# Splitting two more aggregates of a two-layer graph attention kernel a second time, with the residual rows prepared in DRAM

## The chip, the cores and the metric

The kernel runs on one core of a Trainium2 chip. The metric is the device time of one execution in microseconds (us). The profile names the engines PE (TensorE, matmuls; PEld is its weight load), DVE (VectorE), ACT (ScalarE), POOL (GpSimd) and SP (SyncE, here used only to start DMAs). "L661" is line 661 of the kernel before.

## The reference

Two graph attention layers over N = 2708 rows of D = 1024 features, all in float32. Cut to what matters:

```python
# layer 0
h = relu(layernorm(x))
f, g = h @ Wf + bf, h @ Wg + bg
attention = softmax(where(adj > 0, relu(f @ g.T), NEG), axis=1)
x = x + attention @ (h @ W0 + bW)
# layer 1
h1 = relu(layernorm(x))
hw = h1 @ W1
e = leaky_relu(hw @ a1 + (hw @ a2).T, 0.2)
attention = softmax(where(adj > 0, e, NEG), axis=1)
return x + relu(attention @ hw)
```

The kernel multiplies attention by h first (the "aggregate") and by the weight matrix after that (the "projection").

## The kernel before, in words

**Tiling.** The 2708 rows are 20 full tiles of 128 rows, taken as NQ = 10 pairs, or NK = 5 pairs of pairs, and a left-over of two more tiles (MONO with 128 rows, TINY with 20). Destination rows of the attention matrix lie along the free dimension, in NP = 5 panels of 576, 576, 532, 512 and 512 columns (p = 0 to 4).

**Products.** Every large matrix product is a Strassen-Winograd product: seven half-size products M1 to M7, some on operands that are sums of blocks. An operand of one of them that is built from h lies ready in DRAM, and is streamed into SBUF in tiles `hc`; the other, built from the softmax numerators of the panel, is made in SBUF by VectorE. Two functions compute an aggregate:

- `aggregate` computes seven unsplit products with `accumulate` (matmuls at L661). One product is 10 pairs x 4 blocks of 128 features = 40 matmuls of h columns, h being half of the panel's width, and reads five `hc` tiles of 512 KB.
- `aggregate_quartered` splits each of the seven products again, into seven inner products (L1067) of 5 pairs of pairs x 2 blocks = 10 matmuls with h/2 columns. Its operands are the quarter sums of h, which lie in `hs2_d`, and the quarter sums of the attention block, which VectorE makes with `make`. Each partial result is collected from PSUM into a tile `V` and added into `gT` by VectorE. Before the change only layer 1's panels 1 to 4 are computed so.

`quarters_of(p, S)` returns the functions that make the sums of columns (`first`, `fifth`, `second`, `fourth`), and the operands.

**DRAM scratch.** `hg_d` holds the operands of layer 0's aggregates, 4 KB in a row for each partition and load; `hr_d` and `hs2_d` hold those of layer 1 and their quarter sums, in runs of 1 KB for each block. `hs_d` holds transposed rows for the scores, `mk_d` masks, `wt_d` sums of weights, `x1_d` the rows that layer 0 puts out.

**Order.** For each panel of layer 0 the program emits: the projection of h to queries (`project_q`), the scores (`scores`), the aggregate and the projection (`project`). They interleave: the queries of panel p + 1 stand between the scores and the aggregate of panel p. Layer 1 follows: for each panel an aggregate and a projection.

**Side work.** Small pieces of work stand in two lists, `later` and `lazy`, each with an assumed cost. `behind(us)` is called between groups of matmuls: it adds `us` to a credit and takes pieces while credit is left, from `lazy` only where `spare` is set and `later` is empty. A piece's loads (`fetch`) are emitted a few pieces ahead. One such piece is a quarter item (`put_quarters`): it reads 512 KB of `hr_d` into a tile `hq`, makes four sums on VectorE and stores 512 KB to `hs2_d`. `quarters_until(m)` takes pieces until product m's are made.

**Queues and buffers.** `load` starts a DMA on SP's queue in program order; `store` starts one on GpSimd's queue, which a scheduler orders. ScalarE starts no loads of this kind. Tiles of `stream(...)` (`hc`, `hq`, `hl`, `w`, and more) share a ring of `strm` buffers, and a new tile waits for the release of the oldest one. Tiles of `slot(...)` share 54 buffers.

**The residual.** `finish0(p)` loads x's rows of each output tile (`x_res`, two halves, each as four loads of 64 KB) and adds the bias with two accumulating DMAs on GpSimd's queue (256 KB each, L1612). It then adds the projection's result, stores to `x1_d`, and starts layer 1's normalisation of these rows.

Of the kernel before, what the change touches and what calls it, by code (L numbers as in the profile page):

```python
# [57 lines left out]
def kernel(  # L58
# [60 lines left out]
    strm = ctx.enter_context(tc.tile_pool(name="strm", bufs=12))  # L119
# [34 lines left out]
    groups = [[q, q + 1] for q in range(0, NQ, 2)]  # L154
    group_of = {q: (i, j) for i, g in enumerate(groups) for j, q in enumerate(g)}
    assert sorted(group_of) == list(range(NQ))
    hg_d = [dram.tile([P, 7, len(g), W], FP, name=f"hg_d{i}") for i, g in enumerate(groups)]
    NK = NQ // 2
    WH = W // 2
    hr_d = dram.tile([P, 7, 2, 2, NK, WH], FP, name="hr_d")  # L160
    hs2_d = dram.tile([P, 7, 4, NK, WH], FP, name="hs2_d")

    def rows_at(m, q):

        return hr_d[:, m, :, q % 2, q // 2]
# [30 lines left out]
    spare, from_slots = [False], [False]  # L196
# [14 lines left out]
    def behind(us, psum_free=False):  # L211
        credit[0] = min(credit[0] + us, 2 * us)
        while later and credit[0] > 0 and (psum_free or not later[0][3]) and (not later[0][4] or later[0][4]()):
            credit[0] -= one()
        while spare[0] and not later and lazy and credit[0] > 0:
            credit[0] -= one(lazy)
# [107 lines left out]
    def pair_h(q, ha, hb):  # L324
# [3 lines left out]
        if q >= NQ - F // 2:  # L328
            s1, s2, s3, s4 = (slot(f"g{i}")[:, :W] for i in range(4))
            for m, h in ((M1, ha[0]), (M2, hb[0]), (M4, hb[1])):  # L330
                store(rows_at(m, q), as_blocks(h))
            on.tensor_tensor(s1, ha[1], hb[1], OP.add)
            on.tensor_tensor(s2, s1, ha[0], OP.subtract)
            for m, h in ((M5, s1), (M6, s2)):
                store(rows_at(m, q), as_blocks(h))

            def rest():
                on.tensor_tensor(s4, hb[0], s2, OP.subtract)
                on.tensor_tensor(s3, ha[0], ha[1], OP.subtract)
                for m, h in ((M3, s4), (M7, s3)):  # L340
                    store(rows_at(m, q), as_blocks(h))
# [7 lines left out]
        for m, h in ((M1, ha[0]), (M2, hb[0]), (M4, hb[1])):  # L349
            store(rows_at(m, q), as_blocks(h))  # L350
        store(rows_at(slice(M5, M6 + 1), q), as_blocks(g1[:n]))
        store(rows_at(slice(M7, M3 + 1), q), as_blocks(g2[:n]))

    def rows_h(q, ha, hb):

        i, j = group_of[q]
        for m, h in ((M1, ha[0]), (M5, ha[1]), (M2, hb[0]), (M4, hb[1])):
            store(hg_d[i][:, m, j], h)
# [3 lines left out]
    def sums_h():  # L362

        def fetch(q, two):
            i, j = group_of[q]
            for m in (M1, M2):
                two.append(stream("hr", (P, 2, W)))
                load(two[-1], hg_d[i][:, m:m + 2, j])
# [6 lines left out]
        def second(q, two):  # L375
# [3 lines left out]
            i, j = group_of[q]  # L379
            store(hg_d[i][:, M6:M7 + 1, j], two[0])  # L380
            store(hg_d[i][:, M3, j], b0)
            store(hg_d[i][:, M5, j], b1)
# [6 lines left out]
    BY_QUARTERS = (M1, M5, M2, M6, M7, M3, M4)  # L389
    made_quarters = {}  # L390

    def put_quarters(m, k, to=lazy):
# [3 lines left out]
        def fetch():  # L396
# [5 lines left out]
            for h in range(2):  # L402
                nc.gpsimd.dma_start(two[h], hr_d[:, m, h, :, k])

        def go():
# [5 lines left out]
            for h in range(2):  # L411
                store(hs2_d[:, m, 2 * h:2 * h + 2, k], two[h])
            made_quarters[m] = made_quarters.get(m, 0) + 1
        put(1.7, go, fetch, to=to)

    def quarters_until(m):
        while made_quarters.get(m, 0) < NK:
# [466 lines left out]

    def aggregate(l, p, S, sm, then={}, rate=3.0):
# [28 lines left out]
        def left(m, q, d):  # L914
            i, j = group_of[q]
            if (m, i) not in hc:
                hc[m, i] = stream("hc", (P, 4, WH) if l else (P, 2, W))
                load(hc[m, i], hr_d[:, m, :, :, i].rearrange("p h f c -> p (h f) c") if l else hg_d[i][:, m])
            return hc[m, i][:, d // 2 * 2 + j, d % 2 * P:(d % 2 + 1) * P] if l else hc[m, i][:, j, d * P:(d + 1) * P]
# [67 lines left out]
    def quarters_of(p, S):  # L987
# [9 lines left out]
        def operand(m, q):  # L997
            if m in (M5, M4):
# [30 lines left out]
        def second():  # L1029
            for q in range(NQ):  # L1030
                sub(wa_(q)[:, lo], wb_(q)[:, hi], t1(q))
            for q in range(NQ):
                sub(wa_(q)[:, hi], wb_(q)[:, hi], wa_(q)[:, hi])

        def fourth():
            for q in range(NQ):
                sub(t1(q), wb_(q)[:, lo], wa_(q)[:, lo])
        return {"make": make, "right": right, "first": first, "fifth": fifth, "second": second, "fourth": fourth}

    def aggregate_quartered(p, S, sm, of_right, then={}, fine=1.2):  # L1040
# [12 lines left out]
        def product(m, n, ps, start):  # L1053
            quarters_until(m)
# [782 lines left out]
```

## Time and profile before

| | us |
|---|---|
| median of 3 runs | 3091.45 (3090.53 to 3099.64) |
| the profiled execution, its own time | 3099.78 |
| its span, first to last instruction | 3098.0 |
| TensorE busy | 3002.8 |
| VectorE busy | 2070.7 |
| ScalarE, GpSimd busy | 463.2, 506.3 |
| layer 0's aggregates of panels 1, 2, 3 | 148.1, 137.1, 132.0 |
| layer 1's aggregates of panels 2, 3 | 127.4, 125.0 |

The mean granted TensorE clock is 0.989. The core's DMA queues moved 764.7 MB, 247 GB/s over the span. A busy time is the sum over an engine's instructions; a stage's length is read off the timeline, from its first to its last matmul. The profile's DMA share is the mean busy share of the core's 16 DMA engines in a slice of time, and comes out a few per cent above 1 in the fullest slices. A float32 matmul leaves two records in the trace, so counts of matmul records are twice those of the code.

### The profile page before, as it was taken

Reading aid. Unit: us, or ns where it says so; the run is one execution under the profiler, and the core shown is the slowest. Engines: PE = TensorE matmul, PEld = TensorE weight load, DVE = VectorE, ACT = ScalarE, POOL = GpSimd, SP = SyncE. Lnnn points to the kernel's source line nnn. Section 1 sums busy time; section 2 is a strip of 40 time slices with the busy share of each in tenths; the row PEclk is TensorE's granted clock in tenths of the full one; section 3 lists DMA queues with packets and bytes.
Section 4 is the critical chain, followed back from the end, with each engine's and each line's share of the span. In section 5 each row is a group of like instructions: output and inputs, shape, how many; then the busy total and the mean of one; then the engine's idle time right before and its main releaser. Section 6 shows DMA issues by size and latency. Waiting matters only on the chain.

```text
span 3098.0 us, 41680 instructions
## 1 busy us (share of the span) xinstructions
PE 3002.8 (97%) x14630; PEld 2298.1 (74%) x14630; DVE 2070.7 (67%) x4615; ACT 463.2 (15%) x817; POOL 506.3 (16%) x786
## 2 busy tenths in 40 slices
PE   8998999899999999999999999997999999999998
PEld 4576777657877588885888886783777969879694
DVE  5767693776651596716975277766968768887853
ACT  3420020010110101101011001301222121212200
POOL 1421101310011110214101001141202010020202
PEclk9999999999999999999999999998999999999999
DMA  6999967998565796758967577789667868888896
GB/s 225 291 257 254 301 247 253 309 274 229 178 238 153 217 260 223 244 158 241 278 199 255 164 217 234 237 266 350 229 216 249 274 202 296 287 269 294 264 297 246
DMA packets 448577, 764.70 MB, mean 247 GB/s; under 512 B 175776, under 2 KB 262592, under 8 KB 448368
## 3 DMA queue, kind: packets, MB, share of 16 engines
q1 hardware_dynamic: 393008, 598.31, 62.0%
q0 software_dynamic: 55360, 163.73, 16.4%
q8 instruction: 116, 1.90, 0.3%
q14 instruction: 93, 0.76, 0.1%
HBM read 627.95 MB, written 133.91 MB: 246 GB/s over the span
## 4 chain that ended last, share of the span: by engine, by line
PE 71%; DVE 11%; DMA 7%; issue 7%; SPq 2%; POOL 1%; ACT 1%; POOLq 0%; DVEq 0%; ACTq 0%
PE sz L1378 6%; PE gx L661 6%; PE gy L661 6%; PE gz L661 5%; PE gz L1067 5%; PE pz L1267 4%; PE sx L1378 4%; PE sy L1378 4%; PE px L1267 4%; PE py L1267 3%; PE gx L1067 3%; PE gy L1067 3%; PE M_ps L574 3%; PE qz L661 2%; PE qx L661 2%
## 5 line engine op out<-in xcount | busy, mean ns | idle before, releaser
L1378 PE MATMUL sz<-B,As 128*128 128x288 f32 (+2 forms) x1200 | 293.5, 394 | 11.8 <-DVE st L45 8.8
L1378 PEld LDWEIGHTS sz<-B,As 128*128 128x128 f32 x1200 | 227.8, 191 | 61.8 <-DVE st L45 12.7
L1378 PE MATMUL sx<-B,As 128*128 128x288 f32 (+2 forms) x800 | 199.6, 392 | 6.4 <-DMA As<-hs_d 4.4
L1378 PE MATMUL sy<-B,As 128*128 128x288 f32 (+2 forms) x800 | 199.3, 392 | 2.3 <-DMA As<-hs_d 2.3
L661 PE MATMUL gz<-Sa,hc 128*128 128x288 f32 (+2 forms) x800 | 189.2, 397 | 6.3 <-DMA hc<-hg_d 6.3
L661 PEld LDWEIGHTS gz<-Sa,hc 128*128 128x128 f32 x800 | 153.8, 193 | 40.1 <-DMA hc<-hg_d 6.8
L1378 PEld LDWEIGHTS sx<-B,As 128*128 128x128 f32 x800 | 151.3, 190 | 40.1 <-DMA As<-hs_d 3.7
L1378 PEld LDWEIGHTS sy<-B,As 128*128 128x128 f32 x800 | 152.0, 190 | 33.4 <-issue 2.7
L1067 PE MATMUL gz<-quarter,hc 128*128 128x128 f32 (+2 forms) x1344 | 168.8, 279 | 3.8 <-DVE gT L45 3.7
L143 POOL DMA_DIRECT2D out_dram<-x_res x180 | 89.0, 501 | 482.1 <-DVE x_res L45 474.7
L1067 PEld LDWEIGHTS gz<-quarter,hc 128*128 128x128 f32 x1344 | 160.6, 191 | 5.1 <-DVE gT L45 4.6
L1267 PE MATMUL px<-w,gT 128*128 128x512 f32 x320 | 143.9, 602 | 7.5 <-DMA w<-in_L_gnn_W_dram 6.0
L1267 PE MATMUL pz<-w,ps 128*128 128x512 f32 x320 | 142.1, 594 | 0.8 <-DVE pt L45 0.8
L1267 PE MATMUL py<-w,ps 128*128 128x512 f32 x320 | 142.0, 593 | 0.0
L143 POOL DMA_DIRECT2D mk_d<-mask x55 | 35.8, 652 | 534.8 <-DVE mask L45 528.1
L1267 PEld LDWEIGHTS px<-w,gT 128*128 128x128 f32 x320 | 60.9, 193 | 80.9 <-issue 74.7
L1267 PEld LDWEIGHTS pz<-w,ps 128*128 128x128 f32 x320 | 60.2, 190 | 77.1 <-issue 70.7
L1267 PEld LDWEIGHTS py<-w,ps 128*128 128x128 f32 x320 | 60.5, 190 | 75.8 <-issue 73.9
L574 PE MATMUL M_ps<-wgT,wfT 128*128 128x512 f32 x256 | 113.5, 600 | 1.6 <-ACT hsT L45 1.6
L661 PE MATMUL gy<-T,hc 128*128 128x288 f32 (+2 forms) x480 | 111.6, 394 | 0.0
L977 POOL TENSOR_TENSOR gT<-gT,rr 128x2304 f32<-128x2304 f32 (+5 forms) x12 | 44.4, 3700 | 382.4 <-DVE rr L45 179.8
L661 PEld LDWEIGHTS gy<-T,hc 128*128 128x128 f32 x480 | 91.2, 190 | 19.5
(377 smaller groups left out, 5803.6 us busy)
## 6 DMA issues: line engine op xcount, KB each, us to landing
hc<-hg_d SPq DMA_DIRECT2D x175, 512.0 KB
As<-hs_d SPq DMA_DIRECT2D x150, 512.0 KB
hc<-hr_d SPq DMA_DIRECT2D x119, 512.0 KB
hc<-hs_d SPq DMA_DIRECT2D x112, 512.0 KB
w<-wt_d SPq DMA_DIRECT2D x96, 512.0 KB
w<-in_L_gnn_W_dram SPq DMA_DIRECT2D x72, 512.0 KB
md<-md_d SPq DMA_DIRECT2D x56, 512.0 KB
adj_i<-in_adj_dram SPq DMA_DIRECT2D x200, 128.0 KB
```

What stands on the lines that cost most here:

```text
L143: nc.gpsimd.dma_start(a, b)
L574: nc.tensor.matmul(ps, wfT[a][c // NH][:, c % NH, :], wgT[b][c], start=(c == 0), stop=(c == NC - 1))
L661: nc.tensor.matmul(ps[d], left(m, k, d), right(m, k), start=(start and k == 0), stop=(k == K - 1), skip_group_check=True)
L977: nc.gpsimd.tensor_tensor(of(e, s), of(e, s), by(s, k), OP.mult)
L1067: nc.tensor.matmul(ps[:, d], lhs[:, d * P:(d + 1) * P], inner_right(m, n, k), start=(start and k == 0 and d == 0), stop=(k == NK - 1), ski ...
L1267: nc.tensor.matmul(ps, left[i][m][:, k, :], w_[k], start=(start and k == 0), stop=(k == NH - 1), skip_group_check=True)
L1378: nc.tensor.matmul(ps[:n, :h], lefts[q][:, i % 2, c, :n], B[m][c // 2][:, c % 2, :h], start=(start and c == 0), stop=(c == NH - 1), skip_g ...
```

## The change

1. Layer 0's aggregates of panels 2 and 3 go through `aggregate_quartered`. M1 and M5 stay unsplit there, by way of `accumulate`; the other five products are split into seven inner ones. For layer 0, `V` is one tile of the stream ring, whose buffers grow from 4096 to 4608 bytes a partition; the ring has 11 of them for 12.
2. Layer 0's operands are laid out like layer 1's (`hr_d[0]` for `hg_d`, runs of 1 KB), and have quarter sums of their own (`hs2_d[0]`). Their 25 quarter items enter `lazy` after panel 0's aggregate.
3. During layer 0's aggregates the reads of quarter items, layer 1's among them, are started on ScalarE's queue in program order, instead of on GpSimd's.
4. The residual rows are copied from x to `x1_d` in tile order by DMA from DRAM to DRAM (`copy_residual`, 512 KB a tile as 4 x 32 rows), and the bias is added there by an accumulating DMA (`bias_residual`, 512 KB a tile). `finish0` then needs two loads of 256 KB a tile and no accumulation.
5. `behind` takes at most one piece from `lazy` per call.
6. In `quarters_of`, `second` and `fourth` build their sums in place; the operand of M4 lies in another tile, and `fourth` moves from M2 to M6. Each has as many instructions as before.

The core of the diff:

```diff
-    strm = ctx.enter_context(tc.tile_pool(name="strm", bufs=12))
+    strm = ctx.enter_context(tc.tile_pool(name="strm", bufs=11))
...
-    hg_d = [dram.tile([P, 7, len(g), W], FP, name=f"hg_d{i}") for i, g in enumerate(groups)]
-    hr_d = dram.tile([P, 7, 2, 2, NK, WH], FP, name="hr_d")
-    hs2_d = dram.tile([P, 7, 4, NK, WH], FP, name="hs2_d")
...
+    hr_d = [dram.tile([P, 7, 2, 2, NK, WH], FP, name=f"hr{l}_d") for l in range(2)]
+    hs2_d = [dram.tile([P, 7, 4, NK, WH], FP, name=f"hs2{l}_d") for l in range(2)]
+
+    def rows_at(l, m, q):
+
+        return hr_d[l][:, m, :, q % 2, q // 2]
...
         while later and credit[0] > 0 and (psum_free or not later[0][3]) and (not later[0][4] or later[0][4]()):
             credit[0] -= one()
-        while spare[0] and not later and lazy and credit[0] > 0:
+        if spare[0] and not later and lazy and credit[0] > 0:
             credit[0] -= one(lazy)
...
     def rows_h(q, ha, hb):
 
-        i, j = group_of[q]
         for m, h in ((M1, ha[0]), (M5, ha[1]), (M2, hb[0]), (M4, hb[1])):
-            store(hg_d[i][:, m, j], h)
+            store(rows_at(0, m, q), as_blocks(h))
...
-    BY_QUARTERS = (M1, M5, M2, M6, M7, M3, M4)
+    BY_QUARTERS = [(M2, M6, M7, M3, M4), (M1, M5, M2, M6, M7, M3, M4)]
     made_quarters = {}
 
-    def put_quarters(m, k, to=lazy):
+    def put_quarters(l, m, k, to=lazy):
...
             for h in range(2):
-                nc.gpsimd.dma_start(two[h], hr_d[:, m, h, :, k])
+                (tc.keep_in_program_order(nc.scalar.dma_start(two[h], hr_d[l][:, m, h, :, k])) if reads_by_act[0] else
+                 nc.gpsimd.dma_start(two[h], hr_d[l][:, m, h, :, k]))
...
             for h in range(2):
-                store(hs2_d[:, m, 2 * h:2 * h + 2, k], two[h])
-            made_quarters[m] = made_quarters.get(m, 0) + 1
+                store(hs2_d[l][:, m, 2 * h:2 * h + 2, k], two[h])
+            made_quarters[l, m] = made_quarters.get((l, m), 0) + 1
...
         def operand(m, q):
-            if m in (M5, M4):
+            if m == M5:
                 return t1(q)
             s = wa_(q) if m in (M1, M6, M7) else wb_(q)
...
         def second():
             for q in range(NQ):
-                sub(wa_(q)[:, lo], wb_(q)[:, hi], t1(q))
+                sub(wa_(q)[:, hi], wb_(q)[:, hi], wa_(q)[:, hi])
             for q in range(NQ):
-                sub(wa_(q)[:, hi], wb_(q)[:, hi], wa_(q)[:, hi])
+                add(wa_(q)[:, lo], wa_(q)[:, hi], wa_(q)[:, lo])
 
         def fourth():
             for q in range(NQ):
-                sub(t1(q), wb_(q)[:, lo], wa_(q)[:, lo])
-        return {"make": make, "right": right, "first": first, "fifth": fifth, "second": second, "fourth": fourth}
-
-    def aggregate_quartered(p, S, sm, of_right, then={}, fine=1.2):
+                sub(wb_(q)[:, lo], wb_(q)[:, lo], wa_(q)[:, lo])
+        return {"make": make, "right": right, "operand": operand, "first": first, "fifth": fifth, "second": second, "fourth": fourth}
+
+    def aggregate_quartered(l, p, S, sm, of_right, then={}, fine=1.2, rate=3.0):
 
...
-        before_next = {M1: lambda: make(M5), M5: with_second, M2: lambda: (of_right["fourth"](), make(M6)), M6: lambda: make(M7),
+        before_next = {M1: lambda: make(M5), M5: with_second, M2: lambda: make(M6), M6: lambda: (of_right["fourth"](), make(M7)),
                        M7: lambda: make(M3), M3: lambda: make(M4)}
+        def sums_of_columns():
+            of_right["second"]()
+            inverse.append(inverse_sums(p, sm))
+
+        def collected():
+            if l == 0:
+                t = stream("V", (P, NH, HX))
+                return [t[:, 2 * r:2 * r + 2, :h] for r in range(2)]
+            return [v[:, :, :h] for v in in_pairs("V")]
+
+        if l == 0:
+            hc = {}
+
+            def left(m, q, d):
+                if (m, q // 2) not in hc:
+                    hc[m, q // 2] = four_rows(l, m, q // 2)
+                return hc[m, q // 2][:, d // 2 * 2 + q % 2, d % 2 * P:(d % 2 + 1) * P]
+
+            def first_product(d, ps):
+                nc.scalar.copy(quad(0, lo)[:, d], ps)
+                nc.scalar.copy(quad(1, lo)[:, d], ps)
+            exps_until(NQ)
+            of_right["fifth"]()
+            accumulate(left, of_right["operand"], NQ, h, (M1, M5), then,
+                       {M1: first_product, M5: lambda d, ps: add(quad(0, hi)[:, d], ps, quad(0, lo)[:, d])}, "g",
+                       {M5: sums_of_columns}, rate=rate, by_k=True, more={(M5, NQ // 2): with_second})
+
         left_out = None
-        for m in BY_QUARTERS:
-            V = [quad(*direct[m])[:, 2 * r:2 * r + 2] for r in range(2)] if m in direct else [v[:, :, :h] for v in in_pairs("V")]
+        for m in BY_QUARTERS[l]:
+            V = [quad(*direct[m])[:, 2 * r:2 * r + 2] for r in range(2)] if m in direct else collected()
             c11, c12 = (V[0][:, :, b * hb:(b + 1) * hb] for b in range(2))
             c21, c22 = (V[1][:, :, b * hb:(b + 1) * hb] for b in range(2))
             X = bank2("gx")
@@ -1169,9 +1194,7 @@
                 into_place(m, V, 1)
                 scale(m, 1)
             if m == M5:
-                of_right["second"]()
-            if m == M5:
-                inverse.append(inverse_sums(p, sm))
+                sums_of_columns()
...
                 fetch(q + 2)
+            if p and q in (2, 6):
+                (copy_residual if q == 2 else bias_residual)(p)
             sa, sb = slot("Sa"), slot("Sb")
...
+    def tiles_of(p):
+        return list(full(p)) + ([MONO, TINY][p - 1:p] if p in (1, 2) else [])
+
+    def copy_residual(p):
+        for t in tiles_of(p):
+            if t < MONO:
+                r = places[t][0][1]
+                nc.gpsimd.dma_start(x1_d[t].rearrange("(g r) c -> g r c", g=P // B32),
+                                    bass.AP(tensor=x.tensor, offset=x.offset + r * D, ap=[[P * D, P // B32], [D, B32], [1, D]]))
+            else:
+                for ps, r in places[t][:1] if t == TINY else places[t]:
+                    nc.gpsimd.dma_start(x1_d[t][:NY] if t == TINY else x1_d[t][ps],
+                                        x[r:r + ps.stop - ps.start, :])
+
+    def bias_residual(p):
+        for t in tiles_of(p):
+            n = NY if t == TINY else P
+            nc.gpsimd.dma_start(x1_d[t], bass.AP(tensor=bw.tensor, offset=bw.offset, ap=[[0, n], [1, D]]), accum_op=OP.add)
 
     def finish0(p):
...
                 xs[t] = row_halves("x_res", t == MONO)
-                load_rows_of(t, xs[t], x)
                 for e in range(2):
-                    nc.gpsimd.dma_start(xs[t][e], bias_of_W(e * W, P, W), accum_op=OP.add)
+                    load(xs[t][e], x1_d[t][:, e * W:(e + 1) * W])
...
+    SPLIT_EARLY = (2, 3)
...
-            hooks[M1] = lambda: (take_max(0), sums_until(3))
+            hooks[M1] = lambda: (take_max(0), sums_until(3), copy_residual(0))
+            hooks[M5] = lambda: bias_residual(0)
...
-        spare[0], from_slots[0] = p > 0, p == NP - 1
-        G[p] = aggregate(0, p, S, got["sm"], then)
-        spare[0] = False
+        spare[0], from_slots[0], reads_by_act[0] = p > 0, p == NP - 1, True
+        if p in SPLIT_EARLY:
+            G[p] = aggregate_quartered(0, p, S, got["sm"], quarters_of(p, S), then)
+        else:
+            G[p] = aggregate(0, p, S, got["sm"], then)
+        spare[0] = reads_by_act[0] = False
         if p == 0:
             flush()
+            for m in BY_QUARTERS[0]:
+                for k in range(NK):
+                    put_quarters(0, m, k)
             ahead[0] = 2
...
```

## The prediction

> **What bounds the kernel now.** I read the page from the top: busy times first, then the chain that ended last, then the groups of instructions.
>
> ```profile
> PE 3002.8 (97%) x14630; PEld 2298.1 (74%) x14630; DVE 2070.7 (67%) x4615; ACT 463.2 (15%) x817; POOL 506.3 (16%) x786
> ...
> DMA  6999967998565796758967577789667868888896
> ...
> PE 71%; DVE 11%; DMA 7%; issue 7%; SPq 2%; POOL 1%; ACT 1%; POOLq 0%; DVEq 0%; ACTq 0%
> ...
> L661 PE MATMUL gz<-Sa,hc 128*128 128x288 f32 (+2 forms) x800 | 189.2, 397 | 6.3 <-DMA hc<-hg_d 6.3
> ...
> L1067 PE MATMUL gz<-quarter,hc 128*128 128x128 f32 (+2 forms) x1344 | 168.8, 279 | 3.8 <-DVE gT L45 3.7
> ```
>
> TensorE is idle for 95 of 3098 us: fewer TensorE cycles shorten the kernel one for one where nothing else is late. The DMA row is the second limit: slices of the first half stand at 9, so what is added there may be late. L661 is the unsplit product, L1067 the inner one of a split product.
>
> Next the windows of single stages. Columns: stretch, length, busy time of PE, PEld, DVE, ACT, POOL with their counts, TensorE's clock, DMA share, GB/s. The rows are the layer-0 aggregates of panels 1, 2, 3 (unsplit), the layer-1 aggregates of panels 2, 3 (wholly split, same widths), the end of layer 0, and a stretch of panel 0's scores.
>
> ```profile
> 864.00:1012.10 148.10, 148.10 (x629) 114.15 (x628) 47.90 (x110) 6.05 (x13) 27.81 (x28) 1.00 0.67 199
> 1262.20:1399.30 137.10, 137.10 (x630) 114.18 (x630) 45.21 (x109) 4.80 (x11) 29.24 (x32) 1.00 0.69 208
> 1639.20:1771.20 132.00, 132.00 (x629) 114.16 (x628) 45.19 (x111) 4.24 (x10) 18.92 (x19) 1.00 0.71 217
> 2562.80:2690.20 127.40, 124.73 (x1125) 122.98 (x1124) 102.59 (x283) 23.07 (x43) 4.38 (x10) 1.00 0.87 295
> 2743.10:2868.10 125.00, 122.71 (x1126) 121.23 (x1125) 100.24 (x282) 22.89 (x43) 3.92 (x8) 1.00 0.90 305
> 2085.20:2160.90 75.70, 56.73 (x133) 25.34 (x131) 48.54 (x121) 10.73 (x19) 18.61 (x27) 0.87 1.03 348
> 225.00:290.00 65.00, 55.97 (x238) 42.86 (x237) 48.99 (x113) 7.79 (x15) 12.31 (x22) 0.97 0.97 260
> ```
>
> The unsplit aggregates have a TensorE that never stops and a third of the DMA time free. The split ones lose 2.7 and 2.3 us of TensorE and draw 295 to 305 GB/s. The last two rows are full of DMA with TensorE idle 19.0 and 9.0 us: there, bytes are time.
>
> **What the Trainium skill says.** "DMA: Bandwidth & Descriptors", section "Issuing engines are not separate DMA queues": transfers started by ScalarE, SyncE or GpSimd share the same 16 DMA engines, and another issuing engine saves only sequencer time. So moving the quarter-sum reads to ScalarE's queue frees no bandwidth. The trace agrees in so far as the share tops out at 1.02 to 1.04 whichever queue feeds it (387 GB/s in 880 to 900 us, 398 in 1280 to 1300, 395 in 2100 to 2120). The same page, section "Why a DMA increments its semaphore by 16 and not by 1", says that the number of engines is the largest up to 16 that divides the slowest dimension. The residual copy has 4 there, so 4 engines and some 128 KB each; no transfer of the trace before shows that shape.
>
> **The change part by part.** 0.3% (9.3 us) is about what a measurement of this kernel can tell from no change. Duration rows of the chain of waits:
>
> ```profile
> 1262.40 17.93 PE gx L661 x80
> ...
> 2597.61 4.53 PE gz L1067 x40
> ```
>
> 1. *Five products split in aggregates 2 and 3.* A matmul leaves two records: 80 are one product of 40 matmuls, and the second row is two inner products of 133 columns. Seven inner products cost 7 x 4.53/2 = 15.86 us against 17.93: 2.07 less. At 256 against 128 columns the chain has 17.27 and 4.47: 7 x 2.235 = 15.65, so 1.62 less. Five each: 10.35 + 8.1 = **-18.45 us**, all TensorE time. The left-over tile's matmuls cost the same either way (2.57 to 2.65 against 2.53 to 2.58 us a product): nothing.
> 2. *New waits on VectorE there.* The quarter sums, `collected()` and the scale lie on VectorE: its instructions go from 108 to 248 (panel 2) and 109 to 240 (panel 3), still below layer 1's 282, which took 100 us beside 125. Layer 1 idles 2.67 and 2.29 us, about half at the opening M1 (there is no such wait with M1 unsplit). I take 1.2 each, **+2.4**, bounds 0 and 5.
> 3. *25 more quarter items.* Each reads 0.52 MB, takes four VectorE sums (128x256, 406 ns each) and stores 0.52 MB. The built order puts 22 of them in aggregate 1: 29 items for 7, bytes 28.7 to 54.5 MB, or 368 GB/s over 148.1 us. VectorE gains 22 x 1.6 = 36 on 48 of 148: hidden. ScalarE issues the reads in order with its own work, so they bunch after its PSUM copies, and what is queued behind one is the next copy of sums out of PSUM; those lie 20 and more matmuls later. An `hc` load takes the same ring of 11 buffers as the items, but is issued 30 to 80 matmuls (14 to 37 us) before its use. 368 is under the 387 to 398 of the short stretches: I take **+2**, bounds 0 and 31 (at 305 GB/s, what layer 1 sustained, 54.5 MB take 179 us). Aggregates 2 and 3 go to 43.8 and 40.4 MB, 345 and 326 GB/s: within the same bounds, taken as nothing.
> 4. *Residual rows in DRAM: the end of layer 0.* `finish0` loads two 256 KB halves per tile for eight 64 KB rows and two 256 KB bias accumulations: SP issues 25 loads for 43 in the last projection, and its stages carry 15.5 for 18.1 and 17.0 for 22.1 MB. In the saturated 75.7 us, 5.1 + 2.6 MB at 348 GB/s are 22 us of DMA, but part only moves within it (the aggregates beside them gain 2.3 and 3.5 MB). Net 1.9 MB, 5.5 us; **-6**, bounds -12 and 0, the low end being two thirds of the 19.0 idle.
> 5. *Residual rows: the front.* The diff writes copies and accumulations into scores and panel 0's hooks; in the built order GpSimd's queue carries them earlier. Two 0.5 MB copies (on 4 engines) come at the very start, beside the Wf loads that TensorE waits for (pieces of 9.8, 8.0 and 5.8 us of the chain). They move 2.1 MB; at 400 GB/s 5 us: **+3**, bounds 0 and 6. Four accumulations (2 MB) and a copy go ahead of the last `hs_d` stores of panel 0's scores, where the chain has these rows:
>
> ```profile
> 225.48 11.39 DMA hs_d<-hsT
> ...
> 237.01 6.98 DMA As<-hs_d
> ```
>
> Queued behind them on GpSimd's queue is the `hs_d` store, and behind its landing the `As` load that TensorE waits for. Five issues at 0.9 us (the bias accumulation's, L1612) are 4.5 us, and their 3 MB at 260 to 350 GB/s 9 to 12. TensorE idles there already; **+5**, bounds 0 and 12. The other copies fall into panel 0's aggregate and second half: **+1**, bounds -2 and 5. Panel 0's stages together go from 163.5 to 176.9 MB.
> 6. *Runs of 1 KB for 2 and 4 KB, one lazy item per call, 11 buffers for 12, `second`/`fourth` in place.* Layer 1 reads its 1 KB runs at 305 GB/s with share 0.90, above the 208 to 217 asked here: nothing, but if that cover goes it is the bound of step 3. `second` and `fourth` keep their counts.
>
> Sum: -18.45 + 2.4 + 2 - 6 + 3 + 5 + 1 = -11.05. Against the profiled execution (3099.78 us, span 3098.0) that is 3088.7; it ran 8.3 above the median of 3091.45, so the forecast is **3080**.
>
> **Rivals.** *A, the gain comes whole:* the front's traffic hides in idle TensorE time that is there anyway, and the end of layer 0 gives 8. -18.45 + 2.4 - 8 + 2 = -22: 3069. For it: POOL is 16% busy, and 178 to 300 us is already late for other reasons (adjacency loads on the same chain). Against: those late loads share the bytes.
> *B, front traffic eats it:* steps 3 and 5 near their upper middle (+5, +5, +9) and the end gives only 3: -16 - 3 + 19 = 0, 3091. For it: DMA slices of 9.
> *C, slower, one place:* aggregate 1 becomes DMA-bound. `hc` loads wait for a ring buffer whose quarter item must first be read (4.2 us), summed and stored (6.9 us), and TensorE waits at L661 for `hc`. At 305 GB/s it takes 179 us, +30.6 for +2, and the rest stands at -13: +17.6, 3109. It decides slower once the stage passes 170 us (54.5 MB under 320 GB/s); the break-even is 161 us. For it: 305 is the most that a whole stage sustained. Against: 387 to 398 in 20 us stretches.
> *D, it doesn't do what it says:* the ordered reads or the copies end elsewhere than written. The order shows that in part already (step 5) and it is priced there.
>
> **How the numbers follow.** Forecast 0.38, A 0.21, B 0.18, C 0.20, others 0.03. Faster by over 0.3%: A, nearly nine tenths of the forecast: 0.54. Same: most of B and a rest of the forecast: 0.19. Slower: C, a part of B, others: 0.27. The range must take in A and part of C: **3063 to 3110**; the likeliest case alone is 3072 to 3086.
>
> **What would show it.** Right: aggregates 2 and 3 of layer 0 at about 128 and 125 us; aggregate 1 still near 148 to 150 us with a DMA share over 0.9 and VectorE near 84 us; 2085 to 2160's stretch shorter, with less idle before `w`; a few us more idle at 0 to 40 and at 225 to 290 us. Wrong: `hc<-hr_d` as the releaser of TensorE at L661 with tens of us; VectorE releasing L1067 by more than 5 us in layer 0; ScalarE late at a PSUM copy because a read ahead of it waits for a buffer; a panel-0 stage longer by over 15 us.

## The result, and the profile after

The changed kernel takes 3253.84 us (median of 4 runs, 3250.89 to 3256.90) against 3094.51 us for the kernel before, a ratio of 1.0514 with a 95% interval of 1.0493 to 1.0535. The profiled execution has a span of 3252.9 us, 154.9 above the 3098.0 of before. The forecast was 3080, the range 3063 to 3110, and even the slower rival stood at 3109.

The same lines of the page as before, in the same order (line numbers are the changed kernel's: L655 is the unsplit product, L1065 the inner one, L1401 the scores):

```profile
PE 3018.0 (93%) x15358; PEld 2329.8 (72%) x15358; DVE 2188.8 (67%) x4973; ACT 469.6 (14%) x837; POOL 493.6 (15%) x771
...
DMA  6897888588877879858896798669776877879797
...
PE 73%; DMA 11%; DVE 11%; SPq 2%; issue 2%; ACT 1%; POOL 0%; ACTq 0%; DVEq 0%; POOLq 0%
...
L1065 PE MATMUL gz<-quarter,hc 128*128 128x128 f32 (+2 forms) x1824 | 230.1, 280 | 7.3 <-DVE gT L45 3.7
...
L1401 PE MATMUL sx<-B,As 128*128 128x288 f32 (+2 forms) x800 | 206.4, 402 | 49.7 <-DMA As<-hs_d 49.3
...
L655 PE MATMUL gz<-Sa,hc 128*128 128x288 f32 (+1 forms) x480 | 117.7, 407 | 9.4 <-DMA hc<-hr_d 9.4
```

TensorE's idle time rose from 95.2 to 234.9 us, by 139.7. Its busy time rose too, by 15.2, though the split should take 18.45 away. The 33.6 us that are left over fit matmuls at a lower granted clock (0.967 in the mean for 0.989): -18.45 + 139.7 + 33.6 = 154.9. The 49.3 us on `As` stood at 4.4 before, in this row:

```profile
L1378 PE MATMUL sx<-B,As 128*128 128x288 f32 (+2 forms) x800 | 199.6, 392 | 6.4 <-DMA As<-hs_d 4.4
```

The windows of the stages in the changed kernel: panel 0's scores, panel 1's aggregate, the aggregates of panels 2 and 3, and the end of layer 0 (columns as in the prediction).

```profile
214.90:450.30 235.40, 167.44 (x677) 127.00 (x677) 117.09 (x255) 11.98 (x23) 37.17 (x56) 0.85 0.87 222
992.50:1172.30 179.80, 153.84 (x629) 116.35 (x628) 87.90 (x198) 6.06 (x13) 49.80 (x60) 0.92 0.89 298
1422.50:1561.80 139.30, 131.76 (x993) 124.65 (x992) 85.78 (x249) 8.18 (x21) 14.66 (x22) 0.96 0.89 306
1801.10:1936.30 135.20, 126.88 (x993) 120.48 (x992) 80.81 (x239) 7.58 (x20) 10.66 (x15) 0.97 0.93 294
2248.80:2314.90 66.10, 53.86 (x133) 24.56 (x131) 48.55 (x121) 10.74 (x19) 14.57 (x22) 0.90 0.97 351
```

Read off the timeline, first to last matmul, the stages whose length changed are these. The short end of layer 0 is what change 4 brought (e1 below shows it); the two largest losses lie in stages where TensorE's work is the same as before.

| layer 0, us | before | after | difference |
|---|---|---|---|
| start and panel 0's queries | 213.4 | 209.7 | -3.7 |
| scores, panel 0 | 164.3 | 235.6 | +71.3 |
| queries, panel 1 | 63.5 | 70.4 | +7.0 |
| aggregate, panel 0 | 163.9 | 188.5 | +24.6 |
| projection, panel 0 | 49.3 | 60.2 | +10.9 |
| scores, panel 1 | 152.0 | 170.3 | +18.3 |
| aggregate, panel 1 | 148.3 | 180.0 | +31.7 |
| aggregates, panels 2 and 3 | 137.2, 132.2 | 139.5, 135.4 | +2.3, +3.3 |
| aggregate and projection, panel 4 | 133.7, 58.1 | 132.3, 48.4 | -1.5, -9.7 |

Panel 1's aggregate starts at 992.5 us for 864.0: the stages ahead of it, called the front below, have lost 128.5 us by then. GpSimd's timeline shows what the front meets (start, duration, instruction, count, idle before and what ended it):

```profile
219.07 0.98 POOL L1633 DMA_DIRECT2D x_d<-in_L_gnn_bW_dram  x1
221.86 0.59 POOL L143 DMA_DIRECT2D hs_d<-hsT  x1 [1.81 <-ACT hsT L45]
222.44 2.59 POOL L1633 DMA_DIRECT2D x_d<-in_L_gnn_bW_dram  x3
...
238.94 0.54 POOL L143 DMA_DIRECT2D hs_d<-hsT  x1 [4.05 <-DMA x_d<-in_L_gnn_bW_dram]
245.95 0.54 POOL L143 DMA_DIRECT2D hs_d<-hsT  x1 [6.47 <-DMA x_d<-in_L_gnn_bW_dram]
```

The four accumulations are issued among the `hs_d` stores, and two of those stores then wait on GpSimd for an accumulation to land. The chain shows the `As` load that is under way meanwhile, and TensorE's timeline the matmuls that wait for it:

```profile
223.50 30.66 DMA As<-hs_d
```

```profile
254.29 3.82 PE L1401 MATMUL sx<-B,As 128*128 128x288 f32 x8 [25.75 <-DMA As<-hs_d]
```

A load of 512 KB took 30.66 us, and after the stall of 25.75 us eight records take 3.82 us for 2.10 to 2.21. From 222 to 254 us the DMA share is 0.98 but only 211 GB/s move (264 in the same stretch before).

### The profile page after: what moved, and what is told of

It reads as the page before. It is cut to its first block, busy times and chain, and to the rows that moved or that the text cites. A ratio compares the mean times of both kernels' runs of the same rounds, so it can differ in the third digit from the quotient of the medians.

```text
span 3252.9 us, 43516 instructions
## 1 busy us (share of the span) xinstructions
PE 3018.0 (93%) x15358; PEld 2329.8 (72%) x15358; DVE 2188.8 (67%) x4973; ACT 469.6 (14%) x837; POOL 493.6 (15%) x771
## 4 chain that ended last, share of the span: by engine, by line
PE 73%; DMA 11%; DVE 11%; SPq 2%; issue 2%; ACT 1%; POOL 0%; ACTq 0%; DVEq 0%; POOLq 0%
PE gz L1065 7%; PE sz L1401 6%; PE gx L655 5%; PE pz L1290 4%; PE gy L655 4%; PE gx L1065 4%; PE gy L1065 4%; PE sx L1401 4%; PE sy L1401 4%; PE px L1290 4%; PE py L1290 4%; PE qz L655 3%; PE M_ps L568 3%; PE gz L655 3%; PE gv L655 2%; PE qy L655 2%
## 5 line engine op out<-in xcount | busy, mean ns | idle before, releaser
L1401 PE MATMUL sz<-B,As 128*128 128x288 f32 (+2 forms) x1200 | 296.7, 397 | 32.8 <-DVE Sb L45 16.1
L1401 PEld LDWEIGHTS sz<-B,As 128*128 128x128 f32 x1200 | 229.9, 192 | 84.8 <-DVE Sb L45 17.0
L1401 PE MATMUL sx<-B,As 128*128 128x288 f32 (+2 forms) x800 | 206.4, 402 | 49.7 <-DMA As<-hs_d 49.3
L1065 PE MATMUL gz<-quarter,hc 128*128 128x128 f32 (+2 forms) x1824 | 230.1, 280 | 7.3 <-DVE gT L45 3.7
L1065 PEld LDWEIGHTS gz<-quarter,hc 128*128 128x128 f32 x1824 | 218.9, 192 | 9.1 <-DVE gT L45 4.6
L1401 PEld LDWEIGHTS sx<-B,As 128*128 128x128 f32 x800 | 155.3, 195 | 85.6 <-issue 27.6
L1401 PE MATMUL sy<-B,As 128*128 128x288 f32 (+2 forms) x800 | 202.6, 397 | 12.8 <-DMA As<-hs_d 12.8
L1401 PEld LDWEIGHTS sy<-B,As 128*128 128x128 f32 x800 | 153.6, 193 | 45.1 <-issue 13.4
L45 DVE TENSOR_TENSOR hq<-hq 128x256 f32<-128x256 f32 x212 | 90.7, 452 | 93.4 <-DMA hq<-hr_d 88.9
L143 POOL DMA_DIRECT2D hs_d<-hq x120 | 86.6, 723 | 331.8 <-DVE hq L45 294.1
L655 PE MATMUL gz<-Sa,hc 128*128 128x288 f32 (+1 forms) x480 | 117.7, 407 | 9.4 <-DMA hc<-hr_d 9.4
L655 PEld LDWEIGHTS gz<-Sa,hc 128*128 128x128 f32 x480 | 93.3, 195 | 33.0 <-DMA hc<-hr_d 9.9
L1290 PEld LDWEIGHTS pz<-w,ps 128*128 128x128 f32 x320 | 60.2, 190 | 76.2 <-issue 71.2
L655 PE MATMUL gy<-T,hc 128*128 128x288 f32 (+2 forms) x480 | 112.1, 394 | 0.5 <-DMA hc<-hr_d 0.5
```

Of the source, the lines that this page charges most:

```text
L45: i = f(*a, **k)
L143: nc.gpsimd.dma_start(a, b)
L655: nc.tensor.matmul(ps[d], left(m, k, d), right(m, k), start=(start and k == 0), stop=(k == K - 1), skip_group_check=True)
L1065: nc.tensor.matmul(ps[:, d], lhs[:, d * P:(d + 1) * P], inner_right(m, n, k), start=(start and k == 0 and d == 0), stop=(k == NK - 1), ski ...
L1290: nc.tensor.matmul(ps, left[i][m][:, k, :], w_[k], start=(start and k == 0), stop=(k == NH - 1), skip_group_check=True)
L1401: nc.tensor.matmul(ps[:n, :h], lefts[q][:, i % 2, c, :n], B[m][c // 2][:, c % 2, :h], start=(start and c == 0), stop=(c == NH - 1), skip_g ...
```

## The experiments

Two theories stood at the start. One: the residual rows' transfers cost the front, the quarter items cost panel 1's aggregate, and the two are separate. The other: the 1 KB runs and the smaller ring cost both. The runs e1, e2, e4 to e7, e9, e10, e13 and e14 were executed once each. Stage lengths are those of one profiled execution, whose total can lie some us off the median (e8: 3088.09 for 3095.24). Lines of the edits are shortened.

**Undoing each part (e1, e2, e3).** e1 puts the old `finish0` back, e2 leaves the split and its items out, e3 does both.

```diff
# e1, e3
-            if p and q in (2, 6):
+            if p in IN_DRAM and q in (2, 6):      # IN_DRAM = (); old finish0
# e2, e3
-    SPLIT_EARLY = (2, 3)
+    SPLIT_EARLY = ()                              # and no put_quarters(0, m, k)
```

> Theory 1 (the transfers that prepare the residual rows hold up panel 0's half of layer 0): without them the scores of panel 0 go from 235 back to about 165 us, and the five stages from there to panel 1's scores give back 132 us together; the end of layer 0 loses its 11 us again: about 3132 us. Theory 2 (the 1 KB runs and the 11-buffer ring hold them up): only the scores of panel 0 improve, by up to 70 us, panel 0's aggregate stays near 188 us: 3185 to 3195 us.

> No aggregate of layer 0 is split and layer 0's 25 quarter items are not made; residual preparation stays. Theory: panel 1's aggregate goes from 180 back to 148 us, those of panels 2 and 3 to 137 and 132: about 37 us less, 3216 us. Rival (the residual copies and the layout hold up panel 1's aggregate): it stays above 165 us, total 3225 to 3240 us.

> Neither residual preparation nor the split, only the 1 KB layout, 11 buffers, one lazy item per call, reads on ScalarE's queue. Theory 1: within 6 us of the kernel before (3092). Theory 2: 15 to 60 us above it, with panel 0's aggregate at 175 us or more.

e1: 3161.56 us; panel 1's aggregate starts at 862.1 us, as before, and takes 181.7. The total is 30 above what was expected: with the split and without prepared rows, the projections of panels 1 and 2 pay (69.3 for 62.0 and 68.1 for 53.1), and panel 3's aggregate (137.4). The last projection is back at 60.1. e2: 3218.91; panel 1's aggregate is back at 148.3, those of panels 2 and 3 at 137.2 and 132.2, and the front still loses 130.0. e3: 3101.84 against 3100.50, ratio 1.0003 (0.9994 to 1.0012). The losses are separate, and layout, ring and the one-piece rule together cost nothing in the total. They shift time between stages, though: in e3 panel 0's scores take 175.3 us for 164.3, and the stages just ahead of them and behind them 5.0 and 5.9 less.

**What of the residual rows costs (e4, e5, e6, e10).** e4 leaves out the accumulations, e5 shapes the copies as 32 x 4 rows, e10 does both, e6 puts such copies on SP's queue in the order of the code. The "4 engines" in the expectations is the count that the prediction took from the Trainium skill's page "DMA: Bandwidth & Descriptors", section "Why a DMA increments its semaphore by 16 and not by 1". The rule there has an exception for some copies that GpSimd starts, as these are, and no trace here shows on how many engines a copy lay.

```diff
# e5, e10, e6
-  x1_d[t].rearrange("(g r) c -> g r c", g=P // B32), ... ap=[[P * D, P // B32], [D, B32], [1, D]]
+  x1_d[t].rearrange("(g r) c -> r g c", g=P // B32), ... ap=[[D, B32], [P * D, P // B32], [1, D]]
# e6 also
-                nc.gpsimd.dma_start(x1_d[t] ...
+                tc.keep_in_program_order(nc.sync.dma_start(x1_d[t] ...
```

> Leaves out the accumulating transfers that add the bias to the residual rows; the copies stay. If the accumulations are the cost: panel 0's scores fall from 235 to below 190 us and the whole falls by 80 us or more (3170). If the copies on 4 engines are the cost: panel 0's scores stay above 210 us and the whole falls by less than 40 us (3215 or more).

> The residual copies as 32 x 4 rows of 4 KB for 4 x 32 rows, so that the slowest dimension is 32; bytes, queue and place unchanged. If the copies cost so much because each lies on 4 engines: panel 0's aggregate falls from 188 to below 172 us, panel 0's scores from 235 to about 200, the whole by 50 to 65 us (about 3195). If bytes or GpSimd's queue cost it: all stages within 8 us of the changed kernel, 3240 to 3260 us.

> The copies on SP's queue in program order (32 x 4 rows), so that copies, and the accumulations that depend on them, come where the code puts them. If the early place made panel 0's scores long: these fall from 235 to 165 to 180 us, and the accumulations cost where they are now (panel 1's queries and after), in all 60 to 110 us less than the changed kernel: 3145 to 3190. If place does not matter: panel 0's scores stay above 200, or another stage takes over the whole loss, 3230 or more.

> Leaves out the accumulations of the bias, and the copies are 32 x 4 rows. If copies on 4 engines and accumulations are the whole cost of the residual preparation: the stages up to panel 1's scores return to within 12 us of the kernel before, and the whole to 3121 to 3135 (the split's cost of about 37 us stays, the end of layer 0 gives 11). If the bytes of the copies cost too: 3145 or more.

| | total, us | start of panel 1's aggregate, against before | scores 0 | aggregate 0 | scores 1 |
|---|---|---|---|---|---|
| after | 3253.84 | +128.5 | 235.6 | 188.5 | 170.3 |
| e4, no accumulation | 3193.72 | +74.4 | 202.2 | 186.6 | 159.2 |
| e5, 32 x 4 | 3181.64 | +57.6 | 187.7 | 164.9 | 151.0 |
| e10, both | 3140.23 | +14.7 | 182.5 | 160.9 | 149.7 |
| e6, in order | 3180.62 | +29.7 | 172.8 | 165.0 | 171.8 |

Accumulations cost 54 us with the first shape of copy, 4 x 32 rows (128.5 - 74.4), and 43 with the second, 32 x 4 rows (57.6 - 14.7). With the second shape, about as many bytes of plain copies cost 16.6 (14.7 against the -1.9 of e1). Removing the accumulations shows what they cost, but not how much of it is the rate of the transfers and how much the waits on GpSimd's queue. e4 met neither of its two expectations: accumulations and copies are of one size. The load shown above has a part of both. In e4, without accumulations, it still took 20.24 us for 30.66:

```profile
223.48 20.24 DMA As<-hs_d
```

The runs with the first shape lose 71 and 60 us more than those with the second, and e5's whole falls by 72 us where 50 to 65 were expected. That is not shown to be the shape's doing, because the built order (the order in which the scheduler put the instructions) changed with it: in e5 the 23 copies are issued from 1 to 252 us for 1 to 915, in e10 from 1 to 197 for e4's 1 to 820, and e5's accumulations end at 260 us for 930. Single copies hardly differ. Those issued in the first 150 us landed after 10.0 us in the changed kernel and 9.2 in e5, those from 150 to 450 us after 18.3 and 16.0 (medians). So shape and place together are worth 60 to 71 us, and how they share it stays open. e10's 14.7 and 3140.23 lie between its two expectations.

Busy DMA engines are not the whole of it either. In panel 0's aggregate of the changed kernel, TensorE stalls while the DMA engines are nearly free:

```profile
629.00:648.00 19.00, 11.95 (x32) 8.20 (x32) 3.15 (x7) 0.00 (x0) 1.60 (x3) 0.80 0.30 95
648.00:665.00 17.00, 12.41 (x32) 8.61 (x32) 0.00 (x0) 0.00 (x0) 0.00 (x0) 0.70 0.11 33
```

Four `hc` issues take SP's queue 35.45 us there; the same four take 8.80 in e10. The chain of waits shows a load, sixteen records (eight matmuls), the next load, and so on, as if a single buffer went round. So the order in which the ring's buffers were dealt out may have changed with the copies, and this may be the 24.6 us of that stage (e4, with the first shape, has 186.6 there, e5 and e10 165 and 161). No run changed the dealing alone.

e6 shows that a later place doesn't save the accumulations. Panel 0's scores are at 172.8, near e1's 173.6, but the scores of panels 1 to 4 grow by 19.8, 16.0, 5.8 and 4.1 us, each where its accumulations fall. In panel 1's scores the windows ahead of them, with five plain copies, and during them are:

```profile
690.00:704.00 14.00, 6.26 (x25) 4.07 (x23) 13.10 (x32) 0.00 (x0) 4.37 (x8) 0.94 0.98 296
711.00:729.00 18.00, 9.40 (x39) 7.03 (x37) 9.74 (x19) 0.00 (x0) 0.59 (x1) 0.83 0.96 177
```

At nearly the same DMA share the engines move 177 GB/s for 296, as the profile counts bytes. Many small packets of other loads run beside the accumulations, but GpSimd's queue taken alone agrees: 2.67 MB in 79.2% of the window is 187 GB/s at a full share, and SP's queue ahead of it, with 3.61 MB in 86.1%, is at 299. The five accumulations of 512 KB took 17.2 us to land (median); those of before, of half the size and into SBUF, took 7.5.

**What holds panel 1's aggregate (e7, e9, e13, e14).** Its chain runs through reads of quarter items, and the longest stall of TensorE is this one:

```profile
1122.86 2.29 PE L858 MATMUL sum_ps<-sm,ones 128*128 128x288 f32 x4 [20.77 <-DVE gT L45]
```

VectorE's timeline just ahead of it:

```profile
1101.88 2.58 DVE L45 TENSOR_TENSOR hq<-hq 128x256 f32<-128x256 f32 x6
1118.92 3.52 DVE L45 TENSOR_TENSOR hq<-hq 128x256 f32<-128x256 f32 x8 [14.46 <-DMA hq<-hr_d]
1122.36 1.18 DVE L45 TENSOR_TENSOR gT<-gy,u 128x288 f32<-128x288 f32 x3
```

The collection `gT<-gy,u`, for which TensorE waits, stands behind an item's sums, and these wait 14.46 us for a read. Four runs ask what makes the read late:

```diff
# e7, in put_quarters, around the four sums
+            if l:
# e9, in layer 0's loop
-        from_slots[0] = p == NP - 1
+        from_slots[0] = p in (1, NP - 1)
# e13, in put_quarters
-                nc.scalar.dma_start(two[h], hr_d[l][:, m, h, :, k])
+                nc.sync.dma_start(two[h], hr_d[l][:, m, h, :, k])
# e14, in layer 0's loop
-        reads_by_act[0] = True
+        reads_by_act[0] = False
```

> Leaves out VectorE's four sums in layer 0's 25 quarter items; their reads and stores stay. If panel 1's aggregate is long because VectorE's queue holds the collection of PSUM behind sums that wait for their read: it falls from 180 to below 158 us (3225). If it is the DMA engines or the buffer ring: it stays at 170 us or more (3243 to 3253).

> In panel 1's aggregate the quarter items take buffers of the slot pool, not of the ring that hc shares; bytes unchanged. If the ring is the limit (hc waits for a buffer whose item is not stored): panel 1's aggregate falls from 180 to below 160 us, the whole to about 3230. If the DMA engines are (54.5 MB at about 300 GB/s): it stays at 172 us or more, 3245 to 3255.

> The changed kernel with the reads of the quarter items on SP's queue, among the hc loads, for ScalarE's. If ScalarE's order is what delays them (a read stands behind copies of PSUM that wait for TensorE, and VectorE's sums and the ring's buffers wait for the read): panel 1's aggregate falls from 180 to below 162 us. If the number of bytes or the ring is all: 174 us or more.

> The changed kernel with these reads on GpSimd's queue, as in the kernel before. If ScalarE's order is the delay and GpSimd's free: panel 1's aggregate below 162 us. If GpSimd's queue holds them as well, behind stores that wait for VectorE's sums: 172 to 190 us.

Panel 1's aggregate took 185.1 us in e7 (3256.97 in all), 165.7 in e9 (3220.81), 187.7 in e13 (3239.29) and 191.4 in e14 (3243.83), for 180.0. So the sums' own work is not the cost: in e7 two of layer 1's items, whose sums stay, wait 34.7 us for their reads, and TensorE again 26.63 for `gT`. For this stage the queue of the reads is not the cost either. Buffers of their own saved 14 us, less than e9's first theory asked and more than its second allowed. In the changed kernel SP's queue, which starts the `hc` loads, waits 107.5 us in this aggregate for stores of items and 41.8 for their reads, in e9 not at all for stores and 67.7 for reads. VectorE still waits 56.8 us for reads in e9, for 66.4, now at a DMA share of 0.97:

```profile
972.20:1137.90 165.70, 153.47 (x630) 117.19 (x629) 88.25 (x206) 5.85 (x13) 52.66 (x64) 0.95 0.97 333
```

What is left there, 17 us over 148, fits the bytes: 55.3 MB, where e17 below, with 40.9 MB and slot buffers too, loses nothing. No run shows it alone.

In panel 3's aggregate the queue of the reads does matter. It takes 125.2 us in e13 and 129.1 in e14, for 135.4 in the changed kernel and 135.3 to 137.4 in the seven runs from e1 to e10 that split it with these reads on ScalarE. Here is e13's, to be read against the row from 1801.10 above:

```profile
1795.10:1920.40 125.30, 124.42 (x994) 119.13 (x994) 80.33 (x239) 7.57 (x20) 10.64 (x15) 1.00 0.93 298
```

TensorE idles 0.9 us for 8.3 at the same DMA share of 0.93, with 37.4 MB for 39.8. SP's queue waits 43.1 us for reads and stores of items in the changed kernel and 5.1 in e13. So change 3, the reads on ScalarE's queue, cost 6.3 us there against the old queue (e14), most of the 8.1 that the split saves; in panel 2's aggregate it cost 4.0.

**Fewer bytes (e11, e15, e17).** Only panel 3 is split, the residual is the old one, and `behind` charges an item more credit, so that items spread over five aggregates. e15 moves the reads to SP, e17 takes slot buffers in the aggregates of panels 1 and 2.

```diff
-            credit[0] -= one(lazy)
+            credit[0] -= max(one(lazy), pace[0])   # pace 5.4, 5.5, 20.0 in aggregates 1, 2, 3
-    SPLIT_EARLY = (2, 3)
+    SPLIT_EARLY = (3,)
```

> No residual preparation; only panel 3's aggregate is split, and the quarter items are paced: 17, 15, 4, 8 and 16 in five aggregates for 29, 10, 7, 7 and 7. If crowding of the DMA engines ate the gain: panel 1's and 2's aggregates stay within 2 us of 148 and 137, panel 3's falls from 132 to 124 to 127, the whole 5 us under the kernel before. If the split costs stalls even so: one of these three is 4 us longer, the whole the same as before or slower.

> Only panel 3's aggregate split, items paced, no residual preparation, reads on SP's queue. If ScalarE's order cost the 7 and 12 us in panel 1's and 2's aggregates of the same kernel with reads on ScalarE: they return to within 2 us of 148 and 137, the whole falls from 3135 to 3110 or less. If pacing or bytes did: they stay above 152 and 145.

> As the run with panel 3 alone split, items paced, reads on ScalarE's queue and no residual preparation (3135 us), but in the aggregates of panels 1 and 2 the items take buffers of the slot pool. If the ring is what makes VectorE wait for an item's read, and the collection of PSUM with it: these two aggregates fall from 155 and 149 to within 3 us of 148 and 137; the whole to 3115 to 3120. If the ring has no part: they stay above 153 and 145.

| | ratio to before (95%) | aggregates 1, 2, 3, us |
|---|---|---|
| e11 | 1.0129 (1.0115 to 1.0144) | 155.3, 148.8, 133.5 |
| e15 | 1.0191 (1.0172 to 1.0211) | 168.6, 156.4, 129.7 |
| e17 | 1.0051 (1.0036 to 1.0066) | 148.3, 137.2, 131.1 |

Panel 1's aggregate in e11, and in e17:

```profile
859.10:1014.40 155.30, 151.73 (x630) 115.99 (x629) 64.59 (x150) 6.05 (x13) 37.20 (x42) 0.98 0.81 263
```

```profile
853.00:1001.30 148.30, 148.30 (x630) 114.32 (x629) 71.37 (x159) 5.86 (x13) 41.08 (x48) 1.00 0.86 276
```

With the same pace e17 moves more bytes per second than e11, and TensorE never stops. VectorE's waits for reads of items fall from 50.7 to 14.4 us in this stage. So in e11 it was the ring and not the bytes: an item's buffer is free only after read, sums and store, the next item's read waits for it, VectorE's queue waits for that read, and the collection of PSUM behind it. Slot buffers cut this loop. On SP's queue (e15) the loop costs more still, so ScalarE's order was not what made these two stages long. What e17 still loses lies where 16 deferred items now fall (layer 1's first two aggregates, +7.2 and +6.7) and in the last projection without prepared rows (65.6 for 58.1).

**Towards a faster version (e8, e12, e16, e18).** e8: no split, residual rows in DRAM for panels 3 and 4 alone, copies in order. e12: that, with the bias added in SBUF by GpSimd. e16: by VectorE, after the projection's result. e18: e16 with panel 3 split as in e17, and `V` in slot buffers as well.

```diff
# e12, in start()
-                    nc.gpsimd.dma_start(xs[t][e], bias_of_W(e * W, P, W), accum_op=OP.add)
+                    nc.gpsimd.tensor_tensor(xs[t][e], xs[t][e], bias[:, e * W:(e + 1) * W], OP.add)
# e16, in go() instead
             add(xs[t][e], c, xs[t][e])
+            add(xs[t][e], xs[t][e], bias[:, e * W:(e + 1) * W])
```

> No split, residual rows prepared in DRAM for panels 3 and 4 alone, copies on SP's queue in order in the scores of these panels. Theory (the end of layer 0 gains from fewer loads and accumulations, and what lies in the scores of panels 3 and 4 is hidden): the last projection of layer 0 falls from 58 to 48 us, panel 4's aggregate by 1.5, the whole 0.25 to 0.4% under the kernel before. Rival (the scores of panels 3 and 4 pay for it as panel 0's did): they grow by 5 us or more each, the whole the same or slower.

> As the run with residual rows in DRAM for panels 3 and 4 alone (no split, copies in order), but no accumulating transfer anywhere: GpSimd adds the bias to the rows in SBUF, from a tile that holds it. If the accumulations made panel 3's scores 6 us longer and kept the end of layer 0 crowded: panel 3's scores return to 138 us, the last projection stays at 48, the whole 8 to 13 us (0.25 to 0.4%) under the kernel before. If the copies did: 144 us stay, and the whole is within 0.1%.

> As the run with the bias added in SBUF by GpSimd, but VectorE adds it, just after the projection's result (44 additions of about 0.7 us more for VectorE). There a VectorE instruction of 0.7 us took 10.3 us while GpSimd ran its eight additions in panel 4's scores. If that was the 8.6 us there: panel 4's scores return to 131 us and the whole falls 5 to 9 us further, to 0.4 to 0.5% under the kernel before. If the additions lengthen the end of layer 0 (VectorE is on its chain): it gains 3 us or less.

> The run with the bias added on VectorE and residual rows in DRAM for panels 3 and 4, and on top of it panel 3's aggregate split, items paced and in buffers of the slot pool, V in slots too. If a split pays once the items don't hold up the ring: panel 3's aggregate falls from 132 to 124 to 128 us and the whole 2 to 6 us under the 3086 of that run. If what the items add elsewhere is more than the 8.1 us of TensorE time that the split saves: above 3088.

| | us, and before beside it | ratio (95%) | scores 3, 4 | aggregate 3 | last projection |
|---|---|---|---|---|---|
| e8 | 3095.24, 3096.57 | 1.0000 (0.9990 to 1.0010) | 144.0, 131.9 | 132.2 | 48.4 |
| e12 | 3089.40, 3097.29 | 0.9975 (0.9966 to 0.9983) | 137.1, 139.5 | 132.5 | 48.7 |
| e16 | 3086.31, 3099.24 | **0.9962** (0.9948 to 0.9977) | 140.2, 130.9 | 132.6 | 48.4 |
| e18 | 3089.67, 3094.21 | 0.9983 (0.9977 to 0.9990) | 142.8, 130.9 | 130.1 | 48.4 |

e8 shows the gain at the end (58.1 to 48.4) and, for it, 6.0 us in panel 3's scores, so both its theories hold a part. e12, without accumulations, has 137.1 in these scores, but e16 and e18, also without, have 140.2 and 142.8, so what moves them by a few us stays open. e16 beats both kernels: 0.4% under the one before. Its gain over e12 is smaller than was expected and not clear of the intervals. In e18 panel 3's aggregate gains 2.1 of the 8.1 us (3.0 idle remain), and items deferred into layer 1 take more than that back. A split of layer 0 does not pay in any version tried.

## Why the prediction was wrong, step by step

Two steps failed. Step 5, the residual rows in the front, is off by over 100 us, and step 3, the quarter items in panel 1's aggregate, by 30.

- **Step 1 (the split's TensorE time, -18.45) held.** Inner products take 2.27 us for 20 records in layer 0 too, and e13's 125.2 us in panel 3's aggregate is the forecast's "about 125". In the changed kernel it was eaten in the same stages: idle 7.5 and 8.3 us, and about 5 and 3 more at the lower clock.
- **Step 2 (+2.4, VectorE's new waits) named the wrong waiter.** The idle time there is TensorE's on `hc`, at 306 and 294 GB/s. "Aggregates 2 and 3 ... taken as nothing" was wrong, and not for the number of bytes: e13 idles 0.9 us in panel 3's at 298 GB/s. By the waits of SP's queue the `hc` loads were late because of items, the more so with their reads on ScalarE's queue, which the prediction weighed only for bandwidth and for copies out of PSUM.
- **Step 3 (+2, bounds 0 and 31) failed: 31.7.** Rival C had the right stage and, with 179 us, the length (180.0), but by a mechanism that is only half of it. The step that failed is "VectorE gains 22 x 1.6 = 36 on 48 of 148: hidden". It priced VectorE's work and not its queue: every item puts an instruction there that waits for a read, and the collection of PSUM is behind it. The ring was seen, but asked only whether TensorE's own `hc` came in time. The fear for ScalarE's queue was unfounded for this stage (e13, e14). And "305 is the most that a whole stage sustained" overlooks a row of its own table, 348 GB/s over the 75.7 us at the end of layer 0; e9 held 333 over this stage.
- **Step 4 (-6) held:** -9.7 in the last projection, within its bounds, and e1 with the old residual is at 60.1. The -1.5 of panel 4's aggregate is not this step's: e1 and e3 have 132.3 there too.
- **Step 5 (+3, +5, +1, together at most 23) failed by far: 128.5.** Place and victim were right, the `As` load. But the longest stall was not a load "behind its landing": it was under way already and took 30.66 us itself, for 6.98 before. The price was wrong in two terms. Accumulations were counted as plain bytes (2 MB at 260 to 350 GB/s), and while they run the DMA engines move 177 GB/s where 296 went before; they are worth 43 to 54 us. And the copies were priced by bytes as well (+3 at the start, +1 for the rest), though their shape was noted as one that no trace had shown. With the second shape they are worth 16.6 us, with the first and the built order that came with it 60 to 71 more; shape and order are not told apart. "TensorE idles there already" took idle time as a cover, but what was late there grew later still.
- **Step 6 (nothing) held:** e3, 1.0003. (A misreading on which nothing rests: from 1280 to 1300 us the DMA share is 1.01, under the "1.02 to 1.04".)
- **A term that was missing:** the lower clock after the stalls, the 33.6 us left over above. In panel 1's aggregate, whose matmuls are the same, TensorE's busy time is 153.84 us for 148.10 beside the new idle time. The Trainium skill's page "TensorE: Matmul & The Clock Gate", section "What's actually happening", states half rate after an idle window of about 3.4 us. The trace agrees: 20 records of 133 columns took 4.77 us after a stall of 4.12 us, and 2.43 once the clock was back. A sum of waits must add the slow matmuls that follow each.

## What to carry to other kernels

Price a background item by the longest wait that its instruction can have in an in-order queue, not by its busy time, and ask what stands behind it; if the item's buffer comes from a ring that the main stream shares, it can wait for itself. Price an accumulating transfer, or one of a new shape, from a trace of that kind, and not by its bytes. A high DMA share alone does not tell whether TensorE will wait: at 0.93 it idled 0.9 us in one kernel and 8.3 in another. And each stall brings slow matmuls after it: here about a quarter of the added idle time on top.

## What the runs showed of the hardware that was not expected

- With accumulating DMAs into DRAM the DMA engines stand at a full share and about 0.6 of the rate (177 for 296 GB/s), and one `As` load beside four of them landed after 30.66 us (20.24 without them).
- In e12 a VectorE instruction of 0.69 us took 10.29, as long as a row of eight GpSimd additions:

```profile
1883.14 10.29 DVE L45 SCALAR_TENSOR_TENSOR Sa<-Sa,mask 128x512 f32<-128x512 f32 x1
```

```profile
1883.05 9.83 POOL L1643 TENSOR_TENSOR x_res<-x_res,bias 128x512 f32<-128x512 f32 x8
```

The Trainium skill's page "SBUF — State Buffer", section "SBUF: two separate sides", says that a VectorE instruction with two SBUF inputs and a GpSimd instruction that reads SBUF share a pair of ports, that the one that starts first has it for its whole instruction, and that the other is blocked. The trace agrees, and shows VectorE blocked for eight in a row, and panel 4's scores 8.6 us longer; with the additions on VectorE (e16) they are at 130.9 again.
